# Values of two pairs of heads by seven products of seven products, in a macaron block of FFN, attention and FFN

## The chip, the cores and the metric

The kernel runs on one core of a Trainium2 chip. The time is the device time of one execution in microseconds; the kernel before took 1201.99 us as the median of 3 runs (1200.39, 1201.99, 1202.19). All data are fp32. TensorE (PE) multiplies a stationary 128x128 operand by a moving one into PSUM, VectorE (DVE) and ScalarE (ACT) read PSUM, GpSimd (POOL) works between SBUF tiles, and SyncE (SP) issues the loads.

## What is computed

The reference, cut to what matters: 1024 tokens (4 batches of 256), width 512, 32 heads of 128.

```python
x = x + 0.5 * ffn(layernorm(x), A, B, Wr)      # 64 experts of rank 16, the best 16 gated
x = x + attention(layernorm(x), wq, wkv, wo)
x = x + 0.5 * ffn(layernorm(x), A, B, Wr)

# attention, for each head h of 32 and batch b of 4
q = x @ wq_h; k = x @ wk_h; v = x @ wv_h        # 512 -> 128 each
p = softmax(causal(q @ k.T * scale))            # 256 x 256
out += (p @ v) @ wo_h                           # 128 -> 512
```

## The kernel before

Heads are taken in 16 pairs, and a pair is a period `p` of the attention's loop. Nearly every product of matrices is made by the seven products of Strassen and Winograd: a product of 2x2 blocks needs seven block products in place of eight, of sums of left blocks (`left_sums`, L166 on) and sums of right blocks (`right_sums`, L177 on). `seven` runs these products in the order of `STEPS`: each step makes one product M1 to M7 onto one of three PSUM banks of a pool of five (`ps_mm`) and then calls the reads that are due, which add a bank's contents into the result in SBUF. A step onto a bank that was used before in the same stage must wait for the read of its earlier contents.

Left operands of the projections are the normalised tokens, turned, with their sums: `xop` [128, 7, 8, 256] holds seven outer blocks (for batches 0, 1 against 2, 3, and for the halves of the width) with eight inner blocks each (four stored, four sums of them). `norm_pair` (L451 on) makes the outer blocks from the first FFN's results (DVE, L464 to L470), and `inner_sums` (L447) the inner ones, on DVE, through L171 to L174 of `left_sums`.

For one pair of heads:

- Queries and keys (`make_qk`, L565): two levels, that is seven products of seven products, 49 matmuls with 256 moving columns (L578). They come in four stages of seven steps: a (M1 and M5), b (M2, M6), c (M7, M3), d (M4); reads at L596, L598, L608, L616 and a POOL addition at L625. Weights are loaded by `load_qk` in seven tiles of a pool of eight, and summed on POOL: four sums 512 wide and 28 of 128 (lines L181, L184, L185, L186).
- Values (`make_v`, L643): one level, seven products of four token tiles and two halves of the contraction: 56 matmuls with 128 moving columns (L652). Reads: four copies of 512 columns on ACT (L668) and three adds of 512 on DVE (L666). Weights: `load` brings two 256 KB halves, `sums_of` makes four sums of 256 on POOL.
- Attention proper, for each head and batch, a unit: scores (`probs`, ps, L728, L729), softmax on DVE and ACT, transposes of the probabilities (`attend`, ptp, L769), product with the values (pa, L774, L781), copies on ACT (L771, L788).
- Output projection of the pair before (`project`, L700; po, L706): one level, two halves of 7 steps of 2 matmuls with 256 columns, read by DVE into x (L718); its left sums are `out_sums` on POOL (so).

The order on each engine is written out by hand, as a string of letters for each of the eight units of a period: `v`, `q` and `o` take one step of the next pair's values, the next pair's queries and keys, and the last pair's output projection; `b` is the second half of an attention unit; `f` in the first period takes what is left of the first pair's queries and keys. So in units 0 and 1 the values are made, and in units 2 to 7 query/key and output steps alternate. The first pair's products are made ahead of the loop, beside the end of the first FFN. Loads and weight sums are issued at the points that the code shows (`load_qk` and `sums_of` inside `make_qk`); POOL works them off in that order, and waits with all behind it where one is not ready. A tile pool gives a buffer again when its last reader is done.

```python
UNITS = (
    "vvbvv",
    "vvbv",
    "qoqbqoq",
    "qoqbqoq",
    "qoqbqoq",
    "qoqbqoqoq",
    "qoqbqoqoq",
    "qoqqbqoqq",
)
```

Of the kernel before, what the change touches and what calls it, by code (L numbers as in the profile page):

```python
# [32 lines left out]
def macaron_kernel(  # L33
# [410 lines left out]
    INNER = {"M1": 0, "M2": 1, "M4": 3, "M5": 4, "M6": 5, "M3": 6, "M7": 7}  # L444
    xop = xpool.tile([P, 7, 8, S], F32, tag="xop", name="xop")

    def inner_sums(lo, hi, eng):  # L447
        o = slice(lo, hi)
        left_sums(eng, [xop[:, o, i] for i in range(4, 8)], *(xop[:, o, i] for i in range(4)))

    def norm_pair(work, pair):  # L451

        half, a = divmod(pair[0] // 2, 2)
        sl = slice(2 * a, 2 * a + 2)

        where = [xop[:, 6, k : k + 2, :].rearrange("p a s -> p (a s)") for k in (4, 6)]
        tokens = normed(work, pair, "a", where)
        yield
        for i, xn in enumerate(tokens):
            pt = turned_x(xn, f"a_{pair[i]}").rearrange("p (o c) k -> p o c k", o=2)  # L460
            a11, a12, s3, a22, s1, s2, _ = (xop[:, k, sl, i * P : (i + 1) * P] for k in range(7))
            if half:
                nc.scalar.copy(a22, pt[:, 1])
                nc.vector.tensor_tensor(s3, a11, pt[:, 0], ALU.subtract)  # L464
                nc.vector.tensor_tensor(s2, pt[:, 1], s3, ALU.subtract)  # L465
                nc.vector.tensor_tensor(s1, a22, pt[:, 0], ALU.add)
            else:
                nc.scalar.copy(xop[:, 0:2, sl, i * P : (i + 1) * P], pt)
        if half:
            nc.vector.tensor_tensor(xop[:, 6, sl], xop[:, 1, sl], xop[:, 5, sl], ALU.subtract)  # L470
        elif a:
            inner_sums(0, 2, nc.vector)
# [3 lines left out]
    def load(kind, p):  # L476

        if p >= NG:
            return
        pool = opool if kind == "o" else vpool  # L480
        w = pool.tile([P, HG, 512], F32, tag="w", name=f"w{kind}_{p}", bufs=2)
        if kind == "o":
            nc.sync.dma_start(w, wo_v[:, p * HG : (p + 1) * HG, :])
        else:
            for j in range(HG):
                nc.sync.dma_start(
                    w[:, j, :].rearrange("p (c e) -> p c e", c=DC), wv_v[:, :, p * HG + j]
                )
        raw[kind, p] = w

    def sums_of(kind, p):
        if p >= NG:
            return
        w = raw[kind, p]
        pool = opool if kind == "o" else vpool
        t = pool.tile([P, 3, 256], F32, tag="t", name=f"t{kind}_{p}", bufs=2 if kind == "o" else 1)
        if kind == "o":
            b = [w[:, k, n * 256 : (n + 1) * 256] for k in range(2) for n in range(2)]
        else:
            b = [w[:, n, k * 256 : (k + 1) * 256] for k in range(2) for n in range(2)]  # L500
        rights[kind, p] = right_sums(
            nc.gpsimd, [t[:, i, :] for i in range(3)], *b, pinned=kind == "o" and p == 0
        )

    def load_qk(p):


        if p >= NG:
            return
        w = {  # L510
            m: qkpool.tile([P, 7, P], F32, tag="w", name=f"wqk_{p}_{m}", bufs=8)
            for m in ("M1", "M5", "M2", "M6", "M7", "M3", "M4")
        }
        for m, k, n in (("M1", 0, 0), ("M5", 0, 1), ("M2", 1, 0), ("M3", 1, 1)):
            for i, view in enumerate((wq_v, wk_v)):
                nc.sync.dma_start(
                    w[m][:, i : i + 3 : 2], view[:, 2 * k : 2 * k + 2, p * HG + n, 0:DN]
                )
        right_sums(
            nc.gpsimd,  # L520
            [w[m][:, 0:4] for m in ("M6", "M7", "M4")],
            *(w[m][:, 0:4] for m in ("M1", "M5", "M2", "M3")),
        )
        rights["qk", p] = {
            m: right_sums(
                nc.gpsimd,
                [t[:, i] for i in range(4, 7)],
                *(t[:, i] for i in range(4)),
            )
            for m, t in w.items()  # L530
        }

    with ExitStack() as scope:
# [3 lines left out]
        load("v", 0)  # L537
# [19 lines left out]
    qks, vs, attns = {}, {}, {}  # L557
# [7 lines left out]
    def make_qk(p):  # L565
        if p >= NG:
            return
        right = rights["qk", p]
# [59 lines left out]
        if p > 0:  # L628
            yield from stage(("M1", "M5"), fresh(slice(1, 3)), "a")
            yield from stage(("M2", "M6"), branch(slice(0, 2), 3), "b")  # L630
        else:

            nc.gpsimd.memset(dst[:, 2], 0.0)
            yield from stage(("M1",), fresh(slice(1, 2)), "m")
            yield from stage(("M2",), branch(slice(0, 1)), "n")
            yield from stage(("M6", "M5"), onto(slice(1, 3), 3), "a")
        yield from stage(("M7", "M3"), onto(slice(1, 4, 2), 2), "c")
        if p > 0:
            sums_of("v", p + 1)
        load_qk(p + 1)  # L640
        yield from stage(("M4",), onto(slice(1, 2)), "d")

    def make_v(p):  # L643
        if p >= NG:
            return
        right = rights["v", p]
        dst = vs[p] = pairs.tile([P, NT, HG, DV], F32, tag="v", name=f"v_{p}")

        def product(m, ps, first):
            for t in range(4):  # L650
                for c in range(2):
                    nc.tensor.matmul(  # L652
                        ps[:, t * P : (t + 1) * P],
                        lhsT=xop[:, OUTER[m], t // 2 * 2 + c, t % 2 * P : (t % 2 + 1) * P],
                        rhs=right[m][:, c * P : (c + 1) * P],
                        start=first and t == 0 and c == 0,
                        stop=c == 1,
                        skip_group_check=True,
                    )

        def read(r, ps):
            i, j, adds = READS[r]
            to = dst[:, i * 4 : (i + 1) * 4, j, :]
            of = ps.rearrange("p (t e) -> p t e", t=4)
            if adds:
                nc.vector.tensor_tensor(to, to, of, ALU.add)  # L666
            else:
                nc.scalar.copy(to, of)  # L668

        for i, _ in enumerate(seven(product, read, f"pv_{p}")):  # L670
            if i == 6 and p > 0:
                load("v", p + 1)
            yield
# [87 lines left out]
    def attend(h, b, pr):  # L761
# [6 lines left out]
        for blk in range(3):  # L768
# [7 lines left out]
            lhsT=vs[p][:, 2 * b, j, :],  # L776
# [6 lines left out]
            lhsT=vs[p][:, 2 * b + 1, j, :],  # L783
# [6 lines left out]
    sums_of("v", 0)  # L790
    load_qk(0)
    first_qk, first_v = make_qk(0), make_v(0)
    load("v", 1)
    take(first_v, 2)
    take(first_qk, 7)
    take(first_layer, 1)
    take(first_qk, 7)
    inner_sums(4, 6, nc.vector)
    take(first_v, 3)
    inner_sums(6, 7, nc.vector)  # L800
    inner_sums(2, 4, nc.vector)
    take(first_v, 3)
    take(first_qk, 14)
    sums_of("v", 1)
# [5 lines left out]
        "vvbvv",  # L810
        "vvbv",
        "qoqbqoq",
        "qoqbqoq",
        "qoqbqoq",
        "qoqbqoqoq",
        "qoqbqoqoq",
        "qoqqbqoqq",
# [89 lines left out]
```

## Time and profile before

| | |
|---|---|
| median of 3 runs | 1201.99 us |
| the profiled execution's own time | 1200.26 us |
| its span | 1198.1 us |
| granted TensorE clock | 1.0 throughout |
| first FFN and start, until about 128 us | PE 105.65 busy of the 106.00 us from 22.00 on |
| sixteen periods of attention, steady from the third on | 58.97 us each |
| end of attention and second FFN, from 1082.70 us | PE 112.19 busy of 115.40 us |

Busy durations of instructions on PE overlap: the pace from start to start is what a matmul costs in a full stretch. On the other engines the mean duration is close to the pace.

```profile
L625 POOL TENSOR_TENSOR qk<-qk x128: 716/727/749, 151.4 to 1030.5; 128x256 f32<-128x256 f32 x128
L666 DVE TENSOR_TENSOR v<-v,pv x48: 675/687/689, 131.7 to 991.4; 128x512 f32<-128x512 f32 x48
L668 ACT COPY v<-pv x64: 585/585/589, 129.9 to 993.9; 128x512 f32<-128x512 f32 x64
```

Each of these lines gives minimum, median and maximum of one line's instructions in ns, when the first and the last started, and the shape.

### The profile page before, as it was taken

The page shows a single profiled execution, that of the slowest core. Times are in us where ns is not written, and L with a number is a line of the kernel's source. Part 1 is how long each engine was busy: PE and PEld are TensorE (multiplying, and loading weights), DVE is VectorE, ACT ScalarE, POOL GpSimd, SP SyncE. Part 2 cuts the span into 40 slices and gives each one's busy share as a digit, 9 for nine tenths or more (in the row PEclk, how much of TensorE's full clock was granted, in tenths as well). Part 3 has the DMA queues.
Part 4 walks back from the last instruction along what each step waited for, and adds up shares of the span by engine and source line. Part 5 has one row for each costly group of instructions (what it writes and reads, how often), then busy time and mean ns, then how long its engine had stood idle before and what let it go on. Part 6 is the DMA issues. An engine that isn't in the chain of part 4 may idle for free.

```text
span 1198.1 us, 18680 instructions
## 1 busy us (share of the span) xinstructions
PE 1189.4 (99%) x6716; PEld 1030.0 (86%) x6716; DVE 640.6 (53%) x1722; ACT 503.8 (42%) x1362; POOL 595.0 (50%) x889
## 2 busy tenths in 40 slices
PE   9999999999999999999999999999999999999998
PEld 6667888989898989898989999999999999875767
DVE  5445755373737373646464646464555555675532
ACT  5443225534353434343435343434343434447420
POOL 5316275755646464646473737373838281461110
PEclk9999999999999999999999999999999999999999
DMA  7001211011111111111111111111111000300001
GB/s 250 1 1 36 79 28 36 28 45 34 39 40 33 40 39 37 36 36 36 36 36 36 36 37 36 36 36 36 36 36 36 18 28 1 137 22 1 18 18 35
DMA packets 64426, 47.45 MB, mean 40 GB/s; under 512 B 3920, under 2 KB 55120, under 8 KB 64336
## 3 DMA queue, kind: packets, MB, share of 16 engines
q1 hardware_dynamic: 64336, 46.28, 12.8%
q8 instruction: 53, 0.87, 0.3%
q14 instruction: 37, 0.30, 0.1%
HBM read 44.17 MB, written 2.10 MB: 39 GB/s over the span
## 4 chain that ended last, share of the span: by engine, by line
PE 96%; DMA 1%; ACT 1%; DVE 1%; SPq 0%; POOL 0%; issue 0%; ACTq 0%; DVEq 0%
PE pv L652 17%; PE po L706 16%; PE pqk_c L578 8%; PE pqk_a L578 8%; PE po_f L384 8%; PE pqk_b L578 8%; PE ph_f L318 7%; PE pa L774 5%; PE ps L729 5%; PE pqk_d L578 4%; PE ptp L769 3%; PE ps L728 2%; PE pa L781 2%; PE pth_f L364 1%; PE pr_f L302 1%; DMA wv<-in_wkv 1%
## 5 line engine op out<-in xcount | busy, mean ns | idle before, releaser
L718 DVE TENSOR_TENSOR x<-x,po 128x512 f32<-128x512 f32 x224 | 153.8, 687 | 82.6 <-PE po L706 74.5
L625 POOL TENSOR_TENSOR qk<-qk 128x256 f32<-128x256 f32 x128 | 93.0, 727 | 152.7 <-DVE qk L608 75.3
L737 DVE CUSTOM_DVE_ANT_0 s<-ps,mask 128x128 f32<-128x128 f32 (+1 forms) x256 | 81.4, 356 | 134.6 <-PE ps L729 134.6
L771 ACT COPY pT<-ptp 128x384 f32<-128x384 f32 x128 | 61.5, 480 | 209.8 <-PE ptp L769 209.8
L748 ACT ACTIVATE s<-s,least 128x128 f32<-128x128 f32 (+1 forms) x256 | 114.3, 447 | 68.5 <-DVE least L737 68.5
L652 PE MATMUL pv<-wv,xop 128*128 128x128 f32 x1024 | 124.7, 275 | 0.0
L652 PEld LDWEIGHTS pv<-wv,xop 128*128 128x128 f32 x1024 | 121.1, 192 | 1.1
L758 ACT ACTIVATE s<-s,arden 128x128 f32<-128x128 f32 (+1 forms) x256 | 102.5, 448 | 41.3 <-DVE arden L756 41.3
L578 PE MATMUL pqk_c<-xop,wqk_M 128*128 128x256 f32 x448 | 114.4, 380 | 0.0
L578 PE MATMUL pqk_a<-xop,wqk_M 128*128 128x256 f32 x448 | 114.3, 380 | 0.0
L578 PE MATMUL pqk_b<-xop,wqk_M 128*128 128x256 f32 x420 | 107.3, 379 | 0.0
L181 POOL TENSOR_TENSOR wqk_M<-wqk_M,wqk_M 128x512 f32<-128x512 f32 x16 | 20.3, 1272 | 165.4 <-DMA wqk_M<-in_wkv 107.5
L345 POOL TENSOR_TENSOR hg_f<-hg_f,gate_f 128x512 f32<-128x512 f32 x32 | 33.7, 1057 | 137.7 <-DVE hg_f L331 73.3
L616 DVE TENSOR_TENSOR qk<-qk,pqk_c 128x512 f32<-128x512 f32 x112 | 77.0, 688 | 44.0 <-PE pqk_c L578 29.6
L652 PE MATMUL pv<-tv,xop 128*128 128x128 f32 x768 | 95.0, 276 | 0.4 <-DVE xop L465 0.4
L652 PEld LDWEIGHTS pv<-tv,xop 128*128 128x128 f32 x768 | 91.0, 192 | 1.9 <-DVE xop L465 0.6
L578 PEld LDWEIGHTS pqk_c<-xop,wqk_M 128*128 128x128 f32 x448 | 82.5, 190 | 11.3 <-DVE qk L616 1.5
L578 PEld LDWEIGHTS pqk_a<-xop,wqk_M 128*128 128x128 f32 x448 | 82.5, 190 | 11.0 <-DVE qk L616 0.4
L608 DVE TENSOR_TENSOR qk<-qk,pqk_b 128x512 f32<-128x512 f32 x105 | 72.2, 688 | 31.0 <-PE pqk_b L578 30.8
L578 PEld LDWEIGHTS pqk_b<-xop,wqk_M 128*128 128x128 f32 x420 | 78.7, 190 | 10.1
L788 ACT COPY attn<-pa 128x256 f32<-128x256 f32 x128 | 47.6, 372 | 88.6 <-PE pa L781 88.6
L668 ACT COPY v<-pv 128x512 f32<-128x512 f32 x64 | 37.5, 585 | 102.3 <-PE pv L652 76.1
(161 smaller groups left out, 2464.7 us busy)
## 6 DMA issues: line engine op xcount, KB each, us to landing
wv<-in_wkv SPq DMA_DIRECT2D x32, 256.0 KB, 3.3
wqk_M<-in_wq SPq DMA_DIRECT2D x64, 128.0 KB, 2.3
wqk_M<-in_wkv SPq DMA_DIRECT2D x64, 128.0 KB, 2.5
wo<-in_wo SPq DMA_DIRECT2D x16, 512.0 KB, 3.7
a_f<-in_a_t SPq DMA_DIRECT2D x8, 512.0 KB, 6.2
b_f<-in_b_t SPq DMA_DIRECT2D x4, 1024.0 KB, 9.4
x<-in_x SPq DMA_DIRECT2D x8, 256.0 KB, 8.0
out_x<-x SPq DMA_DIRECT2D x16, 128.0 KB, 1.7
```

The lines of the kernel that those rows point to most:

```text
L318: nc.tensor.matmul(ps, lhsT=left[m][:, c, :], rhs=a_right[m][:, c, :], start=first and c == 0, stop=c == 1, skip_group_check=True,)
L384: nc.tensor.matmul(ps[:, 0:256], lhsT=left[m][:, c, :], rhs=b_right[m][:, c, :], start=first and c == 0, stop=c == 3, skip_group_check=True,)
L578: nc.tensor.matmul(ps[:, i * S : (i + 1) * S], lhsT=right[m][n], rhs=xop[:, OUTER[m], INNER[n]], start=first and i == 0, stop=True, skip_g ...
L608: nc.vector.tensor_tensor(to, of, ps, ALU.add)
L616: nc.vector.tensor_tensor(to, to, ps, ALU.add)
L625: nc.gpsimd.tensor_tensor(to, a, b, ALU.add)
L652: nc.tensor.matmul(ps[:, t * P : (t + 1) * P], lhsT=xop[:, OUTER[m], t // 2 * 2 + c, t % 2 * P : (t % 2 + 1) * P], rhs=right[m][:, c * P : ...
L706: nc.tensor.matmul(ps[:, tt * 256 : (tt + 1) * 256], lhsT=outs[p][m][:, (2 * u + tt) * P : (2 * u + tt + 1) * P], rhs=right[m], start=firs ...
L718: nc.vector.tensor_tensor(to, to, ps.rearrange("p (t d) -> p t d", t=2), ALU.add)
L737: nc.vector.tensor_tensor_reduce(out=s[:, cols], in0=ps[:, cols], in1=mask_f[:, cols], scale=-SCALE, scalar=-TAKEN, op0=ALU.add, op1=ALU.m ...
L748: nc.scalar.activation(s[:, cols], s[:, cols], AF.Exp, bias=least[:, i : i + 1], scale=-1.0, accum_out=den[:, i : i + 1],)
L758: nc.scalar.mul(s[:, cols], s[:, cols], rden[:, i : i + 1])
```

## The change

The values of two pairs of heads (a double pair `k`: pairs 2k and 2k+1) are made together, by two levels: the outer right blocks are the two pairs, the inner ones the two heads of a pair. 49 products of two token tiles each give 98 matmuls with 128 moving columns in place of 2 x 56. They come in stages M1 (a), M2 and M6 (b), M4 and M7 (c), M5 (d), M3 (e), spread over two periods: an odd period makes b and c of the next double pair, an even period d and e, and then a of the one after. The results lie in one buffer `vbuf` of six slots in place of a tile per pair. Their reads take 256 or 512 columns: ACT copies and DVE adds (L721 of the changed kernel, L727, L750), and one POOL addition (L753).

Weights of both kinds go through `two_levels`: five tiles are loaded and summed, and M7's and M4's operands are made in place of M1's and M2's (`t3`, `t4`, POOL, 128x896) once the stages with M1 and M2 are over. The pool of query/key tiles has six buffers in place of eight. Loads of values become 128 KB each.

`xop` keeps seven inner blocks in place of eight: the inner sum of M7 takes the place of the block A21, whose part for the first outer blocks lies in a part of M3's operand (`early`) that is not needed yet. The inner sums of the blocks 2 and 6 move to POOL, 3, 4 and 5 stay on DVE in another order.

The unit strings become two lists, for even and odd periods: value steps alternate with query/key steps from unit 0 on, and output steps come in units 5 to 7 (even) or 4 to 7 (odd). Start and first period have an order of their own. In the last period the output sums are cut in two and their first half is issued a unit earlier, and the second FFN's weight sums are issued two units later.

```diff
-    xop = xpool.tile([P, 7, 8, S], F32, tag="xop", name="xop")
+    xop = xpool.tile([P, 7, 7, S], F32, tag="xop", name="xop")
+    early = xop[:, 5:7, 6]
...
+    def two_levels(pool, bufs, name, blocks):
+        t = {
+            m: pool.tile([P, 7, P], F32, tag="w", name=f"{name}_{m}", bufs=bufs)
+            for m in ("M1", "M5", "M2", "M3", "M6")
         }
         for m, k, n in (("M1", 0, 0), ("M5", 0, 1), ("M2", 1, 0), ("M3", 1, 1)):
+            for i, view in enumerate(blocks(k, n)):
+                nc.sync.dma_start(t[m][:, i : i + 3 : 2], view)
+        def t3():
+            nc.gpsimd.tensor_tensor(t["M1"], t["M6"], t["M1"], ALU.subtract)
+        def t4():
+            nc.gpsimd.tensor_tensor(t["M2"], t["M2"], t["M6"], ALU.subtract)
+        def sums():
+            plain = {m: v[:, 0:4] for m, v in t.items()}
+            nc.gpsimd.tensor_tensor(plain["M5"], plain["M5"], plain["M1"], ALU.subtract)
+            nc.gpsimd.tensor_tensor(plain["M6"], plain["M3"], plain["M5"], ALU.subtract)
+            right = {
+                m: right_sums(
+                    nc.gpsimd, [v[:, i] for i in range(4, 7)], *(v[:, i] for i in range(4))
                 )
+                for m, v in t.items()
+            }
+            right["M7"], right["M4"] = right["M1"], right["M2"]
+            return right, t3, t4
...
             yield from stage(("M1", "M5"), fresh(slice(1, 3)), "a")
+            t3()
             yield from stage(("M2", "M6"), branch(slice(0, 2), 3), "b")
+            t4()
...
+    vbuf = pairs.tile([P, 6, HG, 512], F32, tag="v", name="vbuf", bufs=1)
...
+        def stage(ms, read, name, behind=None):
+            def product(n, ps, first):
+                for i, m in enumerate(ms):
+                    for t in range(2):
+                        nc.tensor.matmul(
+                            ps[:, i * S + t * P : i * S + (t + 1) * P],
+                            lhsT=xop[:, OUTER[m], INNER[n], t * P : (t + 1) * P],
+                            rhs=right[m][n],
+                            start=first and i == 0 and t == 0,
+                            stop=True,
+                            skip_group_check=True,
+                        )
...
+        return {
+            "M1": stage(("M1",), m1, "a", t3),
+            "M2": stage(("M2",), onto_copy(slice(0, 1)), "n", t4),
+            "M6": stage(("M6",), onto(one), "o"),
+            "M2M6": stage(("M2", "M6"), onto_copy(slice(0, u + 1, u)), "b", t4),
+            "M4M7": stage(("M4", "M7"), m47, "c"),
+            "M5": stage(("M5",), onto(slice(u, u + 2)), "d"),
+            "M3": stage(("M3",), onto(one), "e"),
+        }
...
     def make_v(p):
+        k = p // 2
+        if p % 2:
+            yield from chain(*(v_by[k + 1][m] for m in ("M2M6", "M4M7") if v_by[k + 1]))
+        else:
+            yield from v_by[k]["M5"]
+            load_v(k + 1)
+            v_by[k + 1] = v_stages(k + 1)
+            yield from v_by[k]["M3"]
+            if v_by[k + 1]:
+                yield from v_by[k + 1]["M1"]
...
-    first_qk, first_v = make_qk(0), make_v(0)
-    load("v", 1)
-    take(first_v, 2)
-    take(first_qk, 7)
-    take(first_layer, 1)
-    take(first_qk, 7)
-    inner_sums(4, 6, nc.vector)
-    take(first_v, 3)
-    inner_sums(6, 7, nc.vector)
-    inner_sums(2, 4, nc.vector)
-    take(first_v, 3)
-    take(first_qk, 14)
-    sums_of("v", 1)
+    first_qk = make_qk(0)
+    first_v = chain(*(v_by[0][m] for m in ("M1", "M2", "M6", "M4M7")))
+    for _ in range(7):
+        take(first_v, 1)
+        take(first_qk, 1)
+    take(first_layer, 1)
+    for _ in range(7):
+        take(first_v, 1)
+        take(first_qk, 1)
+    inner_sums(5, 6, nc.vector)
+    inner_sums(4, 5, nc.vector)
+    inner_sums(2, 3, nc.gpsimd)
+    inner_sums(6, 7, nc.gpsimd)
+    for _ in range(7):
+        take(first_v, 1)
+        take(first_qk, 1)
+    inner_sums(3, 4, nc.vector)
+    take(first_qk, 7)
...
     UNITS = (
+        (
+            "vqvqbvqvq",
+            "vqvqbvqvq",
+            "vqvqbvqvq",
+            "vqvqbvqvq",
+            "vqvqbvqvqvq",
+            "vooqboq",
+            "voqoqboqo",
+            "voqooqbooqoq",
+        ),
+        (
+            "vqvbqvq",
+            "vqvbqvqv",
+            "qqqbvqvq",
+            "vqvbvqvqv",
+            "qoqoboq",
+            "qoqoqboq",
+            "qoqobqo",
+            "qoqobqoqo",
+        ),
     )
+    FIRST_UNITS = ("gfgfbgf", "gfgfbgfgf", "gvqvqbvqvq", "vqvqbvqvqvq", "vqvqbvqvqvq", "vqvqbvqq", "vqvqbqvqq", "vqvqbvqqq")
...
+            if last and unit == 0:
+                out_sums(p - 1, ((0, 256, nc.gpsimd),))
             if unit == last and p > 0:
-                out_sums(p - 1, ((0, 512, nc.gpsimd),))
+                out_sums(p - 1, ((256 if last else 0, 512, nc.gpsimd),))
...
-        for k in "qvo":
+        for k in "fgqvo":
             take(streams[k], 100)
```

## The prediction, made before the changed kernel ran

> **What bounds the kernel now.** I read the page's busy shares first, then the chain of work that ended last, then busy time by stretches, then the timeline of single instructions inside a stretch.
>
> ```profile
> PE 1189.4 (99%) x6716; PEld 1030.0 (86%) x6716; DVE 640.6 (53%) x1722; ACT 503.8 (42%) x1362; POOL 595.0 (50%) x889
> PE 96%; DMA 1%; ACT 1%; DVE 1%; SPq 0%; POOL 0%; issue 0%; ACTq 0%; DVEq 0%
> ```
>
> TensorE is busy 99% of the 1198.1 us span and makes 96% of the chain; the value products (pv, L652) alone are 17% of the chain. Since the share is an average, I ask it of each stretch. Columns: window, its length, busy time of PE, PEld, DVE, ACT, POOL, granted clock, DMA share, GB/s.
>
> ```profile
> 128.10:169.00 40.90, 40.52 (x263) 35.68 (x262) 29.18 (x60) 10.31 (x25) 19.48 (x30) 1.00 0.22 65
> 271.17:330.14 58.97, 58.97 (x357) 53.84 (x356) 31.80 (x81) 25.09 (x72) 33.04 (x53) 1.00 0.13 37
> 1038.00:1082.70 44.70, 42.46 (x225) 35.10 (x224) 28.80 (x79) 26.16 (x76) 28.62 (x19) 1.00 0.26 95
> ```
>
> The middle line is one period (one pair of heads) of the steady part: 58.97 us long, 58.97 us of PE, at full clock, with DVE at 54% and POOL at 56%. The other two are the start of attention and its end, where PE has gaps. What does a value matmul cost in that full stretch? Busy durations overlap, so I take the pace, start to start.
>
> ```profile
> 515.35 0.60 PE L729 MATMUL ps<-qk 128*128 128x256 f32 x2
> 515.78 1.95 PE L652 MATMUL pv<-tv,xop 128*128 128x128 f32 x16
> 517.57 0.39 PE L652 MATMUL pv<-wv,xop 128*128 128x128 f32 x2
> ```
>
> Sixteen records (each matmul leaves two) start 1.79 us before the next group: 223.4 ns for a 128-column matmul. The same reading gives 432.5 ns for a 256-column one (the tail's timeline below has 0.87 per two) and 1.645 us for a unit's scores, transposes and attention product. Sum of a period: 56 value matmuls x 0.2234 = 12.51, 49 query/key x 0.4325 = 21.19, 28 output x 0.4325 = 12.11, 8 units x 1.645 = 13.16; together 58.97, the measured length. So PE never waits in the steady part, and what leaves PE there leaves the time, unless a wait takes its place.
>
> **The change, part by part.** *Fewer value products.* Before, two pairs of heads cost 2 x 7 products x 4 token tiles x 2 halves = 112 matmuls of 128 columns; after, 49 products x 2 token tiles = 98. Over eight double pairs 896 become 784; all other products keep their number. 112 x 223.4 ns = **-25.0 us**, 3.13 per two periods.
>
> *More reads of PSUM.* Before: 64 ACT copies (128x512, 585 ns) and 48 DVE adds (128x512, 687). After: 64 ACT copies of 256 (372, by the row L788), 129 DVE adds of 512 and 126 of 256 (415, row L616 of pqk_d). DVE gets 129 x 0.687 + 126 x 0.415 - 33.0 = +108 us over the kernel; a steady period gets a sixteenth, 6.7, and goes from 31.8 to about 38.5 of 57.4 us (67%). ACT loses 14 us. Some of the new adds read one block for two outputs: repeated in SBUF that is L608 (688 mean) already; repeated in PSUM (the values' M5 stage) no row shows it. Its bounds are 687 (no effect) and 830 (two of 415); I take 687, by L608. At 830, seven of them per double pair, a period gains 0.5 us of DVE. [...] two 256-wide adds take 143 ns longer than one of 512, 18 us over 126 of them. [...] by the period's rows DVE had 27 us idle of 59, so it is 0 on the path. I take 0.
>
> What hides the reads is the spacing of products. A bank is used again by its stage only after the read, and the letters of a unit now put a query/key step between two value steps: cover 0.446 + 0.865 + 0.446 = 1.76 us. Before, query/key products had 1.52 us (output step and attention product) with DVE 77% busy in those units, and PE did not wait. In the fullest unit after, the reads and the softmax need 4 x 0.415 + 4 x 0.687 + 1.04 = 5.45 of 6.9 us of DVE. So 0 in the steady part; softmax, queued behind reads on DVE, has a whole unit before its transposes.
>
> *Short covers.* The even periods end with output steps back to back (0.865 cover), which the tail already does:
>
> ```profile
> 1068.57 0.59 PE L706 MATMUL po<-wo,attn 128*128 128x256 f32 x2
> 1069.08 0.73 PEld L706 LDWEIGHTS po<-to,attn 128*128 128x128 f32 x4 [0.32 <-DVE x L718]
> 1069.08 1.13 PE L706 MATMUL po<-to,attn 128*128 128x256 f32 x4
> ...
> 1070.05 1.03 PE L706 MATMUL po<-wo,so 128*128 128x256 f32 x4
> ...
> 1070.99 1.13 PE L706 MATMUL po<-to,attn 128*128 128x256 f32 x4
> ```
>
> Steps start 0.97 and 0.94 apart where PE's own pace is 0.865; with the late restart that is about 0.18 us for each step with such a cover. Two per even period from the third on, 14, and one in the last query/key stage: **+2.7 us** (0 to 5).
>
> *POOL's weight sums.* Values now need three sums per weight block: per double pair 2 x 1.272 + 20 x 0.459 + 2 x 2.085 = 15.9 us (896 wide lies between the rows 1272 for 512 and 2356 for 1024) and 4 additions of 0.727, against 2 x 5.8 before (half widths). Query/key: 2 of its 512-wide and 8 of its 128-wide sums become two 896-wide ones, about equal. A period has 33.0 to 39.1 of 57.4 us on POOL. Two 896-wide sums now sit in place behind stage 1 and stage 2 of the same weights, so POOL waits there for PE with its queue (other weight sums, the query/key additions L625, which DVE's L616 waits for) behind it. Followed through the queue, the tightest is the values' second: PE frees the tile at about 14.7 us of the odd period, the stage that uses it starts 4.2 us later, the sum takes 2.1 and POOL is free by then: 1.9 us slack, so 0.
>
> *Loads.* SP issues 64 more halves instead of 32 wholes for the values (128 KB, 2.3 to 2.5 us to land), and the number of query/key tiles drops from 8 to 6, so some loads wait longer for a free tile; they wait only on stages already over, and rows show sums waiting for 107.5 us in total on loads without PE waiting. 0.
>
> *The start of attention.* From 127.9 on, with no values yet and no units to hide behind. Before, 33.85 us pass for 31.56 us of PE work: 2.3 lost. After, three parts add up. The first two value stages begin with an ACT copy that the next product needs (about 0.6 us each, 1.2). DVE is behind with the last token tiles when the second stage's reads fall due: three operations of 0.42 and half of L470 (0.34), up to those, a slowed L470 (1.54) and a read of 0.69: 1.6 to 3.5. And eight token sums with two SBUF inputs are spread over DVE and POOL while POOL runs weight sums. The row for that:
>
> ```profile
> 141.88 1.27 POOL L181 TENSOR_TENSOR wqk_M<-wqk_M,wqk_M 128x512 f32<-128x512 f32 x1 [6.49 <-DMA wqk_M<-in_wkv]
> 142.17 1.26 DVE L171 TENSOR_TENSOR xop<-xop 128x256 f32<-128x256 f32 x1
> ```
>
> A 256-wide DVE sum took 1.26 us, 0.41 elsewhere, ending with POOL's. [...] Read loosely ("POOL slows DVE") it would touch every new value read; the row of L718, one PSUM and one SBUF operand, speaks against that with POOL 50% busy:
>
> ```profile
> L718 DVE TENSOR_TENSOR x<-x,po x224: 671/687/690, 229.9 to 1079.3; 128x512 f32<-128x512 f32 x112
> ```
>
> Minimum, median and maximum are 671, 687 and 690. Loosely, a tenth of the 255 reads losing 0.85 us each would be 22 us of DVE and some of it PE's; strictly, it costs only the token sums beside a POOL sum: 0 to 2.6 us. I take the strict one. With the 0.6 us that PE waits for token operands (xop, L465) now and will then, 3.4 to 7.9 after against 2.3 before: **+1 to +6, middle +3.4**.
>
> *The end.* The sums of the last output operands are cut in two and issued one unit earlier, where PE waited about 0.6 us: **-0.6** (0 to -0.6). The second FFN's sums of weights are issued two units later, far ahead of their use: 0.
>
> Sum: 1200.26 (the profiled execution's own time) - 25.0 + 2.7 + 3.4 - 0.6 = 1180.8. The median of runs lies 1.73 above the profiled one: **1182.5 us**.
>
> **The rivals.** (1) *Waits in the interleave.* A value stage waits on its reads half the time: 140 of the 280 value steps at about 0.06 us, or DVE's queue in the fullest units, makes 8 more, about 1190. For: DVE at 67% with reads in bursts; against: 0.24 us more cover than what sufficed before. (2) *No cost at the start and the short covers fit.* 1202.0 - 25.0 + 0 to 1 = about 1177.5. For: 14 short covers may meet an idle DVE. (3) *Slower.* Every value step waits for its own read as in the tail: 280 steps x 0.18 = 50 us, about 1230. Place: PE's wait on the read of the stage's bank; it decides from 25/280 = 0.09 us per step. For it speaks the tail; against it the spacing, 1.76 us against 0.865. The in-place POOL sum would need to be late by 1.9 + 3.1 us each double pair to do the same. (4) *The change doesn't do what it says.* The compiled order has 784 value matmuls and unchanged others: excluded.
>
> **How the numbers follow.** Forecast 80%, rival 1 10%, rival 2 7%, rival 3 3%. The forecast's own range: 1202.0 - 25.0 + (0 to 5) + (1 to 6) - 0.6 = 1177.4 to 1187.4. The range 1177 to 1191 takes in the other two gaining cases. A change under 0.2% (2.4 us) is about what a measurement of this kernel can't tell from none. Only rival 3 ends there or above: faster 0.95, same 0.02, slower 0.03.
>
> **What would show it.** Right: a steady pair of periods near 114.8 us (117.9 before) with PE full; DVE near 38 us per period; output adds still 687; PE gaps of 3 to 8 us between 128 and 169; value matmuls at 223 ns pace. Wrong: PE waiting on the value reads in the middle (rival 1 or 3), on a POOL sum of 896 columns, or on a weight load; 896-wide sums far from 2.1 us; the first period ending less than 1.6 us earlier, or much more. A gain over 25 us would mean that PE's matmul counts do not set the time as I say.

## The result and the profile after

The changed kernel took 1187.71 us (median of 4, 1187.22 to 1187.91) against 1201.19 (median of 4 runs of the kernel before, 1199.88 to 1202.19): 0.9888 of it, interval 0.9871 to 0.9905. It gained 13.5 us where 19.5 were forecast (1182.5, range 1177 to 1191). The changed kernel run a second time took 1185.23 (the last experiment below).

The page of the changed kernel, busy time and chain, which answer to the first two lines shown of before:

```profile
PE 1166.3 (98%) x6492; PEld 1005.8 (85%) x6492; DVE 741.7 (63%) x1932; ACT 492.7 (42%) x1364; POOL 676.3 (57%) x933
PE 95%; DVE 2%; DMA 1%; ACT 1%; issue 0%; POOL 0%; SPq 0%; DVEq 0%; ACTq 0%
```

PE has 23.1 us less to do, but DVE, 1% of the chain before, is now 2% of it: somewhere PE waits for DVE. Where, the starts of the periods tell (the first scores product of each eighth unit in the timeline):

| stretch | before, us | after, us | difference |
|---|---|---|---|
| first FFN, to the first value product | 127.94 | 130.28 | +2.34 |
| from there to the start of the third period | 142.41 | 152.35 | +9.94 |
| twelve steady periods | 707.75 | 688.70 | -19.05 |
| period 14 | 58.64 | 52.65 | -5.99 |
| the last period and the second FFN | 161.36 | 161.55 | +0.19 |
| span | 1198.10 | 1185.53 | -12.57 |

The steady part and period 14 save all that was counted; two stretches before them give half of it back. Busy time by stretches of the changed kernel (window, length, PE, PEld, DVE, ACT, POOL, granted clock, DMA, GB/s):

```profile
130.28:149.71 19.43, 17.11 (x113) 15.56 (x112) 15.84 (x40) 6.97 (x17) 11.35 (x13) 1.00 0.20 68
149.71:156.64 6.93, 0.83 (x7) 0.43 (x5) 6.93 (x8) 0.00 (x0) 5.59 (x4) 0.90 0.00 0
156.64:163.00 6.36, 6.36 (x22) 5.54 (x23) 3.93 (x8) 0.00 (x0) 0.72 (x1) 0.58 0.00 0
282.63:338.55 55.92, 55.92 (x328) 50.42 (x327) 37.47 (x96) 24.63 (x72) 36.95 (x54) 1.00 0.13 36
338.55:397.41 58.86, 58.86 (x356) 53.82 (x355) 38.21 (x93) 24.20 (x72) 38.40 (x54) 1.00 0.14 39
```

The last two rows are a steady double period: PE full, 114.78 us (117.96 before), DVE 37.47 and 38.21, POOL 36.95 and 38.40. The second row is the place of the loss: in 6.93 us PE works 0.83 and DVE all of it. The third row follows: PE is busy throughout, but at 0.58 of its clock. The timeline of PE there:

```profile
149.94 0.60 PE L835 MATMUL ps<-qk 128*128 128x256 f32 x2
156.64 1.22 PE L696 MATMUL pv_o<-wv_M,xop 128*128 128x128 f32 x4 [6.10 <-DVE vbuf L721]
157.65 3.62 PE L607 MATMUL pqk_a<-xop,wqk_M 128*128 128x256 f32 x8
```

A product of the values' M6 stage waits 6.10 us for a read of its bank (each matmul leaves two records). The eight query/key records after it start within 3.41 us, from 157.65 to 161.06; at the pace of the steady part they take 1.73. From 156.64 to 162.84 the slow clock costs 2.7 us in all: 6.20 us pass for records that take 3.49 at the steady pace. What DVE did meanwhile:

```profile
147.71 1.73 DVE L171 TENSOR_TENSOR xop<-xop 128x256 f32<-128x256 f32 x2
149.35 0.95 DVE L172 TENSOR_TENSOR xop<-xop 128x256 f32<-128x256 f32 x1
150.22 0.94 DVE L174 TENSOR_TENSOR xop<-xop 128x256 f32<-128x256 f32 x1
151.08 2.29 DVE L173 TENSOR_TENSOR xop<-xop 128x256 f32<-128x256 f32 x1
153.29 2.29 DVE L172 TENSOR_TENSOR xop<-xop 128x256 f32<-128x256 f32 x1
155.50 0.41 DVE L174 TENSOR_TENSOR xop<-xop 128x256 f32<-128x256 f32 x1
155.84 0.41 DVE L173 TENSOR_TENSOR xop<-xop 128x256 f32<-128x256 f32 x1
156.17 0.41 DVE L721 TENSOR_TENSOR vbuf<-vbuf,pv_o 128x256 f32<-128x256 f32 x1
```

Eight token sums take 8.46 us, from 147.71 to 156.17. At the pace of the last two, which start 0.33 to 0.34 apart, they would take 2.7 (the expectations below say 3.0). Behind them stands the read that PE waits for. And POOL, for the two sums of 2.29:

```profile
150.84 2.25 POOL L521 TENSOR_TENSOR wv_M<-wv_M,wv_M 128x896 f32<-128x896 f32 x1
153.05 2.24 POOL L521 TENSOR_TENSOR wqk_M<-wqk_M,wqk_M 128x896 f32<-128x896 f32 x1
```

Each of these two sums ends 0.28 us after the POOL operation that was running when it came up (153.37 after 153.09, 155.58 after 155.29), as the one row of before did (143.43 after 143.15).

### The profile page after: what moved, and what is told of

Its sections match the earlier page's. It is cut to its first block, busy times and chain, and to the rows that moved or that the text cites. A ratio compares the mean times of both kernels' runs of the same rounds, so it can differ in the third digit from the quotient of the medians.

```text
span 1185.5 us, 18545 instructions
## 1 busy us (share of the span) xinstructions
PE 1166.3 (98%) x6492; PEld 1005.8 (85%) x6492; DVE 741.7 (63%) x1932; ACT 492.7 (42%) x1364; POOL 676.3 (57%) x933
## 4 chain that ended last, share of the span: by engine, by line
PE 95%; DVE 2%; DMA 1%; ACT 1%; issue 0%; POOL 0%; SPq 0%; DVEq 0%; ACTq 0%
PE po L812 16%; PE pqk_c L607 8%; PE po_f L384 8%; PE pqk_a L607 8%; PE pqk_b L607 8%; PE ph_f L318 7%; PE pa L880 5%; PE ps L835 5%; PE pv_c L696 4%; PE pqk_d L607 4%; PE pv_b L696 4%; PE ptp L875 4%; PE ps L834 2%; PE pa L887 2%; PE pv_a L696 2%; PE pv_d L696 2%
## 5 line engine op out<-in xcount | busy, mean ns | idle before, releaser
L654 POOL TENSOR_TENSOR qk<-qk 128x256 f32<-128x256 f32 x128 | 92.7, 728 | 67.7 <-DVE qk L645 34.0
L607 PE MATMUL pqk_a<-xop,wqk_M 128*128 128x256 f32 x448 | 116.9, 385 | 0.0
L181 POOL TENSOR_TENSOR wo<-wo 128x256 f32<-128x256 f32 x16 | 11.7, 728 | 128.0 <-DMA wo<-in_wo 112.6
L607 PEld LDWEIGHTS pqk_a<-xop,wqk_M 128*128 128x128 f32 x448 | 78.7, 194 | 6.5
L607 PEld LDWEIGHTS pqk_b<-xop,wqk_M 128*128 128x128 f32 x420 | 72.9, 191 | 6.1
L835 PE MATMUL ps<-qk 128*128 128x256 f32 x256 | 76.5, 381 | 0.0
L880 PE MATMUL pa<-pT,vbuf 128*128 128x256 f32 x256 | 76.2, 379 | 0.0
L812 PE MATMUL po<-wo,so 128*128 128x256 f32 x256 | 66.8, 383 | 1.7 <-DVE so L171 1.7
L812 PE MATMUL po<-to,attn 128*128 128x256 f32 x256 | 66.2, 381 | 0.9 <-DVE x L824 0.9
L607 PE MATMUL pqk_d<-xop,wqk_M 128*128 128x256 f32 x224 | 66.3, 380 | 0.0
```

The source lines that it names most:

```text
L607: nc.tensor.matmul(ps[:, i * S : (i + 1) * S], lhsT=right[m][n], rhs=xop[:, OUTER[m], INNER[n]], start=first and i == 0, stop=True, skip_g ...
L654: nc.gpsimd.tensor_tensor(to, a, b, ALU.add)
L812: nc.tensor.matmul(ps[:, tt * 256 : (tt + 1) * 256], lhsT=outs[p][m][:, (2 * u + tt) * P : (2 * u + tt + 1) * P], rhs=right[m], start=firs ...
L835: nc.tensor.matmul(ps[:, P : 3 * P], lhsT=qT[:, P : 2 * P], rhs=kT, start=True, stop=True)
L880: nc.tensor.matmul(po[:, 0 : 2 * P], lhsT=v_of(p, j, 2 * b), rhs=pT[:, 0 : 2 * P], start=True, stop=False,)
```

## Theories

**The theory:** the steady part behaves as predicted. The start of attention loses because token sums with two SBUF operands stand before the reads of PSUM in DVE's queue and are stretched by POOL's sums; PE then waits for a bank, and the idle time costs it the clock. **Rivals:** the mere number of DVE operations at the start is too much; PE really waits for token operands or weight sums; the clock falls for another reason; and, for the steady part, the order of the letters has no share in it.

## The experiments

All of them are edits of the changed kernel and leave out nothing of the reference. Each ratio is to the kernel before, run on the same chip.

**Is it the interleaving that keeps the steady part free of waits?** Same steps, value steps first in a run:

```diff
-            "vqvqbvqvq",
+            "vvvvbqqqq",
```

(and so on in units 0 to 4 of even, 0 to 3 of odd periods.)

> Only the letters of the units from period 1 on: the same steps in each unit, but the value steps first in a run and the query/key steps after them (vvvvbqqqq for vqvqbvqvq). Theory (the steady part has no waits because a query/key step lies between two value steps): a step whose bank's read has only one other step as cover waits: about 0.37 us for the 12 of an even period's 21 value steps that follow a short one, 0.1 for 8 longer ones of the odd period, 0.13 for 16 of 28 query/key steps in each, some 9 us per double period, 7 of these: 1187.7 + 60 = about 1248, slower than the kernel before. Rival (the bank pool of five and DVE's free time hide it in any order): 1188 to 1192.

Measured: 1202.86 us, ratio to before 1.0012 (1.0005 to 1.0019): the whole gain is gone, and a little more. Two periods:

```profile
339.50:399.42 59.92, 59.92 (x357) 53.40 (x355) 38.30 (x93) 24.45 (x72) 38.38 (x54) 1.00 0.14 39
399.42:456.58 57.16, 57.16 (x329) 50.01 (x327) 37.66 (x96) 24.26 (x72) 37.11 (x54) 1.00 0.13 35
```

117.08 us against 114.78. In these rows PE counts as busy all the time, since a short wait hides in the overlapping durations; the starts show it. One output step of the changed kernel, as an example:

```profile
335.45 1.03 PE L812 MATMUL po<-to,attn 128*128 128x256 f32 x4
336.39 1.13 PE L812 MATMUL po<-wo,so 128*128 128x256 f32 x4
337.36 1.03 PE L812 MATMUL po<-to,attn 128*128 128x256 f32 x4
```

Free of waits, such steps start 0.865 apart. Here it is 0.94 and 0.97: the step starts 0.08 us late and its second record a further 0.10, so it loses 0.18. In the changed kernel this is the only late step of the two periods. With the letters in runs, 15 steps of values and of queries and keys are late besides, by 0.08 to 0.25 us each, 2.2 us together. So the theory holds in its sign, and its size was too large mainly by the count: 15 steps wait where 52 were expected, and one costs 0.15 on average where it was 0.1 to 0.37. The rival's 1188 to 1192 is out. Of the 18.5 us between the profiles of this run and of the changed kernel run again, 14.7 lie in periods 2 to 14; the rest is in the first two periods (2.3, a wait of 1.5 us on a sum of 896 columns above all) and at the end (1.7, half clock).

**Does the clock follow the wait?** A first attempt put 24 products of zeros near the wait:

```diff
-    for _ in range(7):
+    for step in range(7):
+        if step == 3:
+            spare = ps_t.tile([P, 512], F32, tag="pt", name="spare")
+            for _ in range(24):
+                nc.tensor.matmul(spare[:, 0:P], lhsT=zeros, rhs=zeros, start=True, stop=True)
```

> 24 products of zeros (128 columns, 0.223 us each, 5.4 us) are added where PE waits in the start of attention; no other work changes. Their results are not used. Theory of the clock (the half clock for 6.8 us, which costs 3.4, follows from PE's idle time): granted clock full there, 1187.7 - 3.4 = 1184.3, or up to 1 us above, since some zeros can push real products. Rival (the half clock has another cause, or is not what costs): 1187.5 or slower by what the zeros push.

Measured: 1190.74 us (1189.48 to 1191.05). In the trace 15 of the 24 lie behind the waiting product, so 9 ahead of it (2.0 us, not the 2.7 of which the next expectation speaks; the records of 6 of them are there): up to 5.74 us of wait and the half clock stay, and the zeros are paid on top. It tells nothing about the clock. The zeros were then pinned ahead of the waiting step:

```diff
-    for _ in range(7):
+    for step in range(7):
+        if step == 2:
+            spare = ps_t.tile([P, 512], F32, tag="pt", name="spare")
+            for _ in range(24):
+                zero = nc.tensor.matmul(spare[:, 0:P], lhsT=zeros, rhs=zeros, start=True, stop=True)
+                tc.keep_in_program_order(zero)
+            with tc.issue_after(zero.ins):
+                take(first_v, 1)
+                take(first_qk, 1)
+            continue
```

> The 24 products of zeros again (5.4 us), their results unused, now fixed in PE's order ahead of the third step of the values' M6 stage, the one that waits 6.1 us in the changed kernel; in the run with the zeros behind it only 2.7 us of them ran before the wait, 5.7 us of wait and 6.8 us of half clock stayed. Theory of the clock: with PE busy there the granted clock stays full, and the start is 3.4 us shorter than in the changed kernel although DVE's sums take as long: third period at 282.6 - 2.3 (the wait in the first FFN, absent in other runs) - 3.4 = about 277, time 1181.5 to 1183. Rival (the half clock comes from elsewhere): third period at about 280.3, 1185.

Measured: 1185.42 us. Busy time in the two stretches that answer to the second and third above:

```profile
148.00:155.80 7.80, 5.94 (x51) 5.70 (x49) 7.80 (x9) 0.00 (x0) 6.46 (x5) 1.00 0.00 0
155.80:163.00 7.20, 6.91 (x38) 5.83 (x39) 6.88 (x15) 0.00 (x0) 1.56 (x2) 1.00 0.01 2
```

The clock is full (1.00 for 0.58) where PE's idle time ahead of that product is 1.86 us in place of 6.10: here it follows PE's idle time. But the time forecast failed: from the first value product to the third period it takes 152.1 us, like the changed kernel (152.0 and 152.4 in its two profiles). The clock had cost 2.3 and 2.7 us in those two (records of 256 columns start 0.43 us apart in place of 0.216), not 3.4, since a part of the half clock falls into the wait itself (in the first of the changed kernel's profiles it begins at 155.20 us, and the wait ends at 156.64). And the pinned order moved a value step of that stage and a unit's scores, 1.1 us which had run before the wait, behind it, with about 1.0 us of small late starts besides (the longest idle time is 0.29). So the cause of the half clock is settled; that removing it gains time isn't shown by this run.

**Is it POOL that stretches the sums?** The two 896-wide sums go behind the query/key additions:

```diff
-        def t4():
-            nc.gpsimd.tensor_tensor(t["M2"], t["M2"], t["M6"], ALU.subtract)
+        def t4(pinned=False):
+            made = nc.gpsimd.tensor_tensor(t["M2"], t["M2"], t["M6"], ALU.subtract)
+            if pinned:
+                tc.keep_in_program_order(made)
...
             yield from stage(("M2",), branch(slice(0, 1)), "n")
-            t4()
             yield from stage(("M6", "M5"), onto(slice(1, 3), 3), "a")
+            t4(True)
...
-            "M2": stage(("M2",), onto_copy(slice(0, 1)), "n", t4),
+            "M2": stage(("M2",), onto_copy(slice(0, 1)), "n"),
+            "t4": t4,
...
+    v_by[0]["t4"](True)
     inner_sums(3, 4, nc.vector)
```

> The changed kernel loses 9.9 us against the kernel before between its first value product and the third period; its trace shows PE idle for 6.1 us at 150.5 while DVE works off eight token sums (xop) in 8.46 us instead of 3.0, beside POOL's own token sums and two 896-wide weight sums, and then half the clock for 6.8 us. Here only the place of the two 896-wide sums changes (behind the query/key additions, when the token sums are over). Theory (DVE's token sums are stretched by what POOL runs at that time): the last five of the eight sums go back to 0.4 to 0.8 us, the eight take 5 us or less, PE's wait falls from 6.1 to about 2.5[...]: 1180.5 to 1183. Rival 1 (the mere number of token sums and reads on DVE is too much): the eight still take over 8 us, 1187.5. Rival 2 (PE waits for operands, whatever the label says): 1187.5 too.

Measured: 1180.45 us, ratio 0.9827 (0.9810 to 0.9843; the changed kernel has 0.9888 and 0.9869 in its two sets of runs). DVE, the last five of the same eight sums, and PE's wait:

```profile
147.90 0.94 DVE L174 TENSOR_TENSOR xop<-xop 128x256 f32<-128x256 f32 x1
148.76 0.41 DVE L173 TENSOR_TENSOR xop<-xop 128x256 f32<-128x256 f32 x1
149.09 0.41 DVE L172 TENSOR_TENSOR xop<-xop 128x256 f32<-128x256 f32 x1
149.43 0.41 DVE L174 TENSOR_TENSOR xop<-xop 128x256 f32<-128x256 f32 x1
149.77 0.41 DVE L173 TENSOR_TENSOR xop<-xop 128x256 f32<-128x256 f32 x1
```

```profile
150.56 0.71 PE L698 MATMUL pv_o<-wv_M,xop 128*128 128x128 f32 x4 [2.35 <-DVE vbuf L723]
```

The two that took 2.29 take 0.41. The eight take 4.7 us in place of 8.46 and PE's wait is 2.35 in place of 6.10: both fall by the same 3.8 us. The half clock lasts 3.4 us instead of 6.8. DVE has the same work in the same order: number alone is out, and so are operands as PE's cause.

**And with no token sum of these blocks on DVE?**

```diff
-    inner_sums(5, 6, nc.vector)
-    inner_sums(4, 5, nc.vector)
+    inner_sums(5, 6, nc.gpsimd)
+    inner_sums(4, 5, nc.gpsimd)
...
-    inner_sums(3, 4, nc.vector)
+    inner_sums(3, 4, nc.gpsimd)
```

> All inner token sums after the first two outer blocks run on POOL (0.72 us each there), none on DVE; everything else as in the changed kernel. Theory (reads of PSUM are late because token sums with two SBUF inputs sit before them in DVE's queue): reads run at 0.41 and 0.69 without interruption, PE's 6.1 us wait goes down to 0 to 2 although the sums themselves are made on the slower engine, and the half clock after it goes: 1177.5 to 1180.5. Rival (PE waits for the token sums themselves): it then waits longer, as 0.72 is above 0.41: 1187 to 1191.

Measured: 1185.17 us (0.9865, 0.9850 to 0.9880), between the two forecasts. The M6 stage has no wait over 0.6 us, as the theory says; but the loss has moved. PE, DVE and POOL of this kernel, by their timelines:

```profile
161.37 7.40 PE L607 MATMUL pqk_c<-xop,wqk_M 128*128 128x256 f32 x20 [6.01 <-DVE qk L645]
```

```profile
160.63 1.48 DVE L645 TENSOR_TENSOR qk<-qk,pqk_c 128x512 f32<-128x512 f32 x2 [6.27 <-POOL qk L654]
```

```profile
157.86 2.06 POOL L521 TENSOR_TENSOR wqk_M<-wqk_M,wqk_M 128x896 f32<-128x896 f32 x1
159.88 2.76 POOL L654 TENSOR_TENSOR qk<-qk 128x256 f32<-128x256 f32 x4
```

Read backwards: PE waits for a read, DVE's read waits for POOL's additions L654, and these stand in POOL's queue behind twenty token sums and the 896-wide sums. The same 6 us, one engine further; the clock falls again. So the next four runs go along POOL's queue.

**Both edits together:**

> Both earlier edits: all inner token sums on POOL and the two 896-wide sums behind the query/key additions. With the sums on POOL alone, the value reads ran undisturbed, but PE waited 6.0 us in stage c for the query/key additions (L654), which stood in POOL's queue behind the token sums and the two 896-wide ones, until 159.9. Theory (it is the queue's order, not the work): the additions start 4.1 us earlier, PE's wait falls to about 2[...]: third period at about 274 (279.95 there), 1178 to 1181. Rival (POOL's work as such is too much for the start): the wait moves to the value products of stage c that need the 896-wide sums, 1184 to 1186.

Measured: 1182.56 us (0.9845, 0.9829 to 0.9862), between the two forecasts again; the wait is 3.99 us, not 2, as the additions still stand behind the last token sums. It shrank by 2.0, and the start took 150.0 us.

**Block 3's sums behind the additions too:**

```diff
             yield from stage(("M6", "M5"), onto(slice(1, 3), 3), "a")
+            inner_sums(3, 4, nc.gpsimd, True)
+            v_by[0]["t4"](True)
             t4(True)
...
-    v_by[0]["t4"](True)
-    inner_sums(3, 4, nc.gpsimd)
```

> As the run with both edits, and the token sums of outer block 3, which are needed last, also go behind the four query/key additions on POOL (2.9 us). Theory: the additions no longer wait for them, no wait over 1 us from the first value product on, full clock: third period at 271 to 273, 1175.5 to 1178; this would be the changed kernel with nearly all of what its products save. Rival: PE then waits for block 3's sums or the 896-wide sums in the first unit, 1179 to 1182.

Measured: 1181.12 us (0.9836, 0.9822 to 0.9851), start 147.0. The wait for the additions is gone and the clock full in the profile, but three waits have come: 0.68 and 0.88 on the 896-wide sums and 1.48 on a value read. The time is the rival's (1179 to 1182), and so are two of the three waits.

**Block 3's sums back on DVE** (the edits of the run with both, but `inner_sums(3, 4, nc.vector)`):

> The token sums of outer blocks 5 and 4, needed first, on POOL; those of block 3, needed last, on DVE as in the changed kernel; the two 896-wide sums behind the query/key additions. Against the run with all on POOL and block 3 behind the additions, POOL has 2.9 us less before the 896-wide sums, for which PE waited 0.68 and 0.88 us there. Theory (POOL's queue order sets those waits; single token sums on DVE cost at most one POOL sum of 0.7 each): no wait over 0.8 us after the copies at the start, full clock, start of attention to third period about 145 us (147.0 there, 152.0 in the changed kernel, 142.4 before): 1178 to 1180. Rival (the token sums on DVE hold up its reads again): 1181 to 1184.

Measured: 1181.51 us (0.9833, 0.9820 to 0.9847), start 147.8. The time is the rival's, but not for its reason. The waits on the 896-wide sums are gone, but one of 2.10 us came, since a query/key read in DVE's queue had stood 3.0 us behind an addition that POOL made after weight sums of the next pair.

**Those weight sums behind the additions,** on top of the edits of the run before:

```diff
-            nc.gpsimd.tensor_tensor(plain["M5"], plain["M5"], plain["M1"], ALU.subtract)
+            first = nc.gpsimd.tensor_tensor(plain["M5"], plain["M5"], plain["M1"], ALU.subtract)
+            if name == "wqk_1":
+                tc.keep_in_program_order(first)
             nc.gpsimd.tensor_tensor(plain["M6"], plain["M3"], plain["M5"], ALU.subtract)
+            with tc.issue_after(first.ins) if name == "wqk_1" else ExitStack():
...
```

> As the mixed run, and the weight sums of the second pair of heads stay behind the eight query/key additions of the first one on POOL. There DVE waited 3.0 us for such an addition, which stood behind weight sums, and PE 2.1 us in turn, followed by half clock for 3.4 us. Theory (what is left of the loss is POOL's order again): that wait goes, the clock stays full from the first value product on, the stretch from there to the third period takes about 145 us (147.8 there): 1178 to 1180. Rival (POOL is simply short of time in the start, any order moves the wait): PE waits for the second pair's sums instead, 1181 to 1183.

Measured: 1177.66 us (1176.41 to 1179.76), ratio 0.9802 (0.9788 to 0.9815). It beats both kernels, and in that stretch PE has no wait over 0.4 us left but those of the two copies and of the M2 stage. The stretch from the first value product to the third period, in this kernel and in the changed one run again:

```profile
129.59:273.37 143.78, 141.32 (x867) 128.15 (x866) 98.36 (x248) 55.58 (x163) 115.25 (x170) 1.00 0.16 44
```

```profile
128.21:280.22 152.01, 143.59 (x867) 130.01 (x866) 107.39 (x256) 55.93 (x163) 110.29 (x162) 0.98 0.15 41
```

143.78 us for 152.01, and 142.41 before the change. DVE is busy 98.4 us for 107.4: eight sums of 0.41 went to POOL, the other 5.7 us are stretching that is gone. POOL has more to do (115.3 us for 110.3) in the shorter time. So POOL is not short of time at the start; its order was wrong.

**Does the first FFN's loss belong to the change?** The changed kernel once more, with no edit:

> The changed kernel itself once more. In its profile the loads of the first FFN's weights landed 1.1 us later than in the kernel before, PE waited 3.4 us and ran 3.4 us at half clock, 2.3 us in all; its four variants do not show this, though they share the code of that part. If it belongs to the single executions and not to the change: clock 0.997 and 1185 to 1185.7. If it belongs to the change: 1187.5 again.

Measured: 1185.23 us (1184.55 to 1185.66), 0.9869 (0.9854 to 0.9883). The step in question, first in the profile after, then in this run:

```profile
21.75 0.84 PE L364 MATMUL pth_f<-ident,hg_f 128*128 128x128 f32 x4 [2.54 <-POOL hg_f L345]
```

```profile
21.02 0.66 PE L364 MATMUL pth_f<-ident,hg_f 128*128 128x128 f32 x4 [1.82 <-POOL hg_f L345]
```

The same wait, 0.7 us shorter, and no half clock behind it; the first value product is at 128.21 (127.94 before). So the loss isn't in the program as such. In the eleven profiles that share this part the wait runs from 1.37 to 2.96 us (1.42 in the one profile of before), with half clock behind it in four. The kernel before spreads as well: of its 48 runs beside the experiments (1199.87 to 1203.08) 19 lie above 1201.5, and 16 of these show a mean clock of 0.998 or 0.999; none of the other 29 does. What makes the wait longer or shorter stays open: the first four runs of the changed kernel (1187.22 to 1187.91) and these four (1184.55 to 1185.66) don't overlap, so it isn't chance from run to run alone. The rest of the loss, 6.1 us of wait with half clock, is in both profiles of the changed kernel.

## Why the prediction was right, and where it was not

- **Fewer products, -25.0 us: right.** Twelve steady periods and period 14 save 25.04. The steady double period was forecast at 114.8 and measures 114.78.
- **Reads on DVE, nothing on the path: right.** 37.5 and 38.2 us per period (forecast 38.5), 512-wide adds from PSUM at 683 to 689 ns in the mean with POOL at 65%; repeated operands cost nothing extra (values' M5 stage, 683).
- **The interleaving hides them: right**, and it decides: in runs, the steps give back 2.3 of the 3.2 us of each double period.
- **Short covers, +2.7 us: right in the price of 0.18, wrong in the count.** One of the two output steps of each even period is late, not both, and one step of the last query/key stage: eight steps, 1.4 us for 15 steps and 2.7. In the total even this is hidden. In the kernel before, one value step of each period started 0.11 us late, 1.4 us over these thirteen periods, which the new order doesn't lose. The prediction's paces added up to the measured 58.97, so it took PE to be free of waits there; it was so but for this 0.11.
- **POOL's sums, no wait of PE: right in the steady part.** The 896-wide sums measure 2090 to 2110 ns (2085 estimated), a steady period 37 to 38 us of POOL (39.1 forecast). The 39.1 doesn't follow from its own terms. The values' sums of before take 4 x 0.727 us per pair, so 2 x 2.9 and not 2 x 5.8; and 2 sums of 512 and 8 of 128 columns (6.2 us) give way to two of 896 (4.2), which is 2.0 less and not "about equal". Put in, they give 37.5.
- **The end, -0.6: wrong.** The wait on L172 is gone, one on L171 grew from 0.7 to 1.7 us; +0.2 in all. It is the collision of the start once more, between DVE's first sum of the last output operands and a weight sum of the second FFN on POOL. DVE and POOL, first before, then after:

```profile
1064.64 1.35 DVE L171 TENSOR_TENSOR so<-attn 128x256 f32<-128x256 f32 x1 [0.44 <-ACT attn L788]
1063.36 2.36 POOL L186 TENSOR_TENSOR bt_f<-b_f,bt_f 128x1024 f32<-128x1024 f32 x1
```

```profile
1051.09 2.35 DVE L171 TENSOR_TENSOR so<-attn 128x256 f32<-128x256 f32 x1 [0.44 <-ACT attn L894]
1050.82 2.34 POOL L186 TENSOR_TENSOR bt_f<-b_f,bt_f 128x1024 f32<-128x1024 f32 x1
```

  The DVE sum ends 0.28 us after POOL's in both; after the change it comes up 1.0 us earlier in POOL's. The prediction set these weight sums at 0, as far ahead of their use. This wait of 1.6 to 2.0 us is in all profiles after, and in three of them (the zeros behind the wait, the runs of letters, the fastest kernel) it took the clock along, which made their end 1.7 us longer.
- **The start, +1 to +6: wrong by its size,** 9.9 us. By the starts of its records, PE loses 12.7 us there against the steady pace; before the change it lost 2.7. The two copies cost 1.25 (1.2 forecast), the M2 stage's late reads 1.6 (1.6 to 3.5). The term that failed is "eight token sums", 0 to 2.6 us: I priced collisions one by one, and took the ends of the sums to be off PE's path. They stand in one block in front of the reads, and all but the last two collide, two of them with 896-wide sums. That delays the reads by 8.46 less 2.7, or 5.8 us, of the 6.1 that PE waits; where 3.8 us of the delay were taken away, 3.8 us of the wait went. I had put the 896-wide sums into POOL's account and the token sums into DVE's, and had not laid the two side by side. And I had no term for the clock: 2.7 us more.

Of the two readings weighed in the prediction the strict one is borne out: sums with two SBUF inputs were stretched (from 0.41 to as much as 2.29 us), while reads with one operand in PSUM kept 0.41 to 0.42 beside POOL's sums (142.8 to 147.4 us), and the 224 output adds took 669 to 690 ns. As for the clock: in the profile after it was at half for 3.41 us from 22.08 us on and for 6.83 from 155.20 on, and otherwise full up to 1184 us; in the profile before it was full up to 1180. Leaving out the first and last microseconds of each of the twelve profiles, it lasted 3.41 or 6.83 us wherever it fell to half. The waits of PE of 3.99 to 6.11 us went with it each time, and of ten waits between 1.9 and 3.0 us nine did (the tenth, 2.35 in the first FFN of the run with block 3 behind the additions, did not); of those below 1.9 none. The shortest wait that it came with here was 1.9 us.

The sum, once more, against the profiled run's own 1187.66 us: it is 6.9 above the 1180.8 worked out, +6.5 at the start beyond its middle, +2.3 in the first FFN and +0.8 at the end, less 2.7 in the steady part (1.3 of short covers, 1.4 for the late step of before). The median, 1187.71, lies just above the forecast's own 1177.4 to 1187.4. The stated range held it only by the room up to 1191 that was left for rival 1, waits in the interleave, and those did not come. So the saving and the absence of waits in the steady part were understood; that the total fell within the range was in part luck.

## What to carry to other kernels

When a change gives work to an engine that is half idle, look for the places where that work is not spread: here each steady period took 6 us more of DVE at no cost, and one burst of eight operations cost PE a wait of 6.1 us and 2.7 us of clock. Lay the queues of engines whose sums stretch each other side by side in time (one DVE sum took 2.29 us here beside one of POOL's, and 0.41 alone): sums that are cheap in each account collide in the joint one. If a wait moves on to the next engine when you take it away, follow it: the order of a queue, not its load, was what had to change.

## What was not expected of the hardware

A DVE sum with two SBUF inputs did not share the time with POOL's sums. Where one of POOL's was running when it came up, it ended 0.28 to 0.30 us after that one, whatever its length (0.95 beside 0.90, 1.26 beside 1.27, 2.29 beside 2.25 us): so it was for all twelve such sums of L171 to L174 in the profiles of before and after, and for 92 of the 94 sums of tokens and outputs in the twelve profiles; the other two took longer still. Those that met no sum of POOL's took 0.41 to 0.43 us at 256 columns. Which came first decided: a DVE sum that had started 0.23 us ahead of POOL's kept its 0.42, and POOL's took 0.78 in place of 0.73 (166.26 us in the profile after).

And PE's idle time of about 6 us cost 2.3 to 2.7 us more by its clock, a loss that doesn't appear as a wait: the rows show PE busy, at 0.58 of the clock.
